# A macaron block with a selective scan: g^T of both FFNs by vector transposes and DRAM, softplus from its table, a new order

## The chip, the cores and the metric

The kernel runs on one core of one Trainium2 chip. Its engines are TensorE (PE, with PEld for its weight loads), VectorE (DVE), ScalarE (ACT), GpSimd (POOL) and SyncE (SP), which issues all DMAs here. The metric is the device time of one execution in microseconds (us), lower is better. Everything is float32.

## The reference, cut to what matters

The input x is [2, 2048, 1024]: 4096 rows of 1024. Three residual blocks follow each other:

```python
def ffn(x, A, B, W, bias):                       # A [64,16,1024], B [64,1024,16], W [1024,1024]
    vecs = einsum('arh,bsh->bsar', A, x)         # 64 vectors of 16 for each row
    _, idx = top_k(norm(vecs, axis=-1), 4)
    routes = one_hot(idx, 64).sum(-2) / 4        # 4 of 64 entries are 1/4
    v = einsum('bsa,bsar->bsr', routes, vecs)    # 16 numbers for each row
    delta = einsum('bsa,ajr,bsr->bsj', routes, B, v)
    return einsum('bsh,jh->bsj', x, W) + bias + delta

x = x + 0.5 * ffn(layernorm(x))
x = x + attn(layernorm(x))       # delta = softplus(x Wx Wdt + b_dt), then a scan over time:
                                 # h = exp(delta*A) * h + delta*B*x,  y = sum_n h*C, + x*D
x = x + 0.5 * ffn(layernorm(x))
```

The last term of the FFN is a product: with g[row, (r, a)] = v[row, r] * routes[row, a], a row of 1024 numbers, delta = g · wb, where wb is B laid out as [1024, 1024].

## The kernel before, in words

**Tiles.** The rows are cut into 16 chunks of 256 (`TC`), each of two row tiles of 128 (`P`). Every tile passes the first FFN (`ffn("f", c, i)`), every chunk the scan's preparation and the scan (`prepare(c)`, `scans(c)`), and every tile the second FFN (`ffn("g", c, i)`): 64 FFN tiles in all. Each takes three products of [128x1024] by [1024x1024] with the weights wa, ww and wb, which stay in SBUF. One tile's product by one weight is 16 products in the code and 32 matmuls of 128x512 in the profile.

**One FFN tile.** PE multiplies wa into the two banks `pv`; ACT squares them (`square`, L631); DVE sums the squares by route, finds the four largest and marks them (`choose`, L645 to L652), multiplies the marks into the vectors (`routed`, L658) and sums them to v (`total`, L668). POOL forms g from marks and v (`spread`, L677). `turn` transposes g in eight blocks of 128x128 on PE (L560) into two banks, and ACT copies them to `gt` (L565). PE meanwhile multiplies ww into the two banks `po` and then adds gt times wb (L578); `close` (L695) adds the result to the rows on DVE. There is one `g` tile and one `gt` tile.

**Softplus.** `prepare` has PE multiply `wdt` into a bank for two groups of 256 columns at a time (`pz`, L797). ACT takes |z| and max(z, 0) from it (L806, L807), then exp(-|z|) (L819) and, with the other function table, a logarithm (L833); DVE has four passes between them that keep the precision (L822, L827, L830, L836). The result `delta` and its product with x go to DRAM (`put`, L856). `scans` reads each row back eight times side by side (`rep`, L890), ACT forms the decays (L917), DVE the entries and scans (L925, L932), POOL multiplies by C and adds (L945, L964), and PE sums the states (L974).

**The order.** `add` records each step as a task with an engine, an assumed cost, what it reads and writes, the buffers that it takes and gives back (`Place`), and a rank. `Plan.order` plays the tasks through once when the program is built: an engine that is free takes the ready task of the lowest rank, and a DMA's data count as there after an assumed `land`. The order in which tasks begin there is the order in which each engine's instructions are written, and each engine keeps to it on the chip. So an assumed cost has no effect on the chip but through the order. For example:

```python
add("SP", 0.4, put_bc, [(bc, 0)], [(bc_d, 0)], rank=-45.3, take=[bc_d], give=[bc], land=1.2)
```

The products with ww and wb of a tile come when they are ready, ahead of the next tile's wa, by the number of their turn (`products`).

Of the kernel before, what the change touches and what calls it, by code (L numbers as in the profile page):

```python
# [16 lines left out]
P = 128  # L37
# [14 lines left out]

class Place:
# [10 lines left out]
class Task:  # L64
    __slots__ = (
        "eng", "cost", "emit", "rank", "take", "give", "port", "land", "turn", "waits", "users", "n",
        "at",
# [9 lines left out]
class Plan:  # L77
# [15 lines left out]
    def add(  # L93
        self, eng, cost, emit, reads=(), writes=(), rank=0.0, take=(), give=(), port=False, land=0.0,
        turn=None,
    ):
        t = Task()
        t.eng, t.cost, t.emit, t.rank = eng, cost, emit, rank
# [27 lines left out]
    def order(self):  # L126
# [9 lines left out]
        def arrive(t):  # L136
            heapq.heappush(ready[t.eng], (t.rank() if callable(t.rank) else t.rank, t.n))
# [89 lines left out]
def macaron_kernel(  # L227
# [54 lines left out]
    places("stats", 6, [P, 17])  # L282
    places("choice", 2, [P, NA + len(PADS) + RANK])
# [4 lines left out]
    plan.pool("du_d", [dram.tile([D, 2, TC], FP, name=f"du_d{j}") for j in range(6)])  # L288
# [32 lines left out]
    pads = const.tile([P, len(PADS) + 1], FP, name="pads")  # L321
    less = pads[:, len(PADS) :]
    nc.gpsimd.memset(less, -1.5)
    for j, v in enumerate(PADS):
        nc.gpsimd.memset(pads[:, j : j + 1], v)

    marked = []
    for j in range(2):
        norms = const.tile([P, NA + len(PADS)], FP, name=f"norms_{j}")
        nc.gpsimd.tensor_copy(norms[:, NA:], pads[:, : len(PADS)])  # L330
        tops = const.tile([P, 2, 8], FP, name=f"tops_{j}")
        nc.gpsimd.tensor_copy(tops[:, 1, :TOPK], pads[:, :TOPK])
        marked.append((norms, tops))
    plan.pool("marked", marked)
# [72 lines left out]
    def load_all():  # L407
        def one(dst, src, key, us, rank):
            keys = [(*key, h) for h in range(2)] if isinstance(key, tuple) else [key]
            add("SP", us, lambda: nc.sync.dma_start(out=dst, in_=src), [], keys, rank=rank, land=3.6)  # L410

        def big(w_sb, w, name, rank):
# [10 lines left out]
            rank=-1000.0, take=[mean_w])  # L423
# [17 lines left out]
        for w_sb, name, key in ((wa, "wa", "pv"), (ww, "ww", "po")):  # L441
            total = Place("row" if name == "wa" else "delta")
            for k in range(1, KC):
                def gather(k=k, w_sb=w_sb, total=total):
                    t = flat(total)
                    eng = nc.vector if total.pool == "row" else nc.gpsimd
                    eng.tensor_add(t, w_sb[:, 0, :] if k == 1 else t, w_sb[:, k, :])

                add("DVE" if name == "wa" else "POOL", 1.01 if name == "wa" else 2.45, gather, [(name, 0, 0), (name, k, 0)], [(total, 0)], rank=-1000.0,
                    take=[total] if k == 1 else [], port=True)  # L450
# [17 lines left out]
            for h in range(2):  # L468
# [10 lines left out]
                for k in range(KC):  # L479
# [4 lines left out]
                    add("DVE", 0.49, center, [(pt, 0)], [(name, k, h)], rank=-900.0, give=[pt])  # L484
# [6 lines left out]
            [], ["half_bias"], rank=272.6)  # L491
# [15 lines left out]
    def spread_of(x_p, st, factor, rank, after=()):  # L507
# [21 lines left out]
        def root():  # L529
            hv, r, t, q = (st.tile[:, j : j + 1] for j in (14, 15, 16, 12))  # L530
# [5 lines left out]
        add("DVE", 1.95, stats, row(x_p) + list(after), [(st, 0)], rank=-109.8 + rank, take=[st])  # L536
        add("ACT", 2.64, root, [(st, 0)], [(st, 1)], rank=72.4 + rank)

    def normalize(x_p, xn_p, rank, after=()):
# [4 lines left out]
        def scale():  # L544
            r, s = st.tile[:, 15:16], st.tile[:, 16:17]
# [6 lines left out]
    def turn(src, keys, dst, out_keys, rank, take=(), give_src=None):  # L552

        for g in range(2):
# [9 lines left out]
            def act(g=g, pt=pt):  # L564
# [4 lines left out]
                give=[src] if give_src else [])  # L569
            add("ACT", 0.58, act, [(pt, 0)], out_keys(g), rank=-111.3 + rank, give=[pt])  # L570
# [3 lines left out]
    def products(turn_of, ps, h, lhs, w, wn, start, stop, order, take, give, after=()):  # L574
        for k4 in range(KC // 4):
            def pe(k4=k4):
# [12 lines left out]
                [(ps[h], 0)], turn=turn_of, rank=order, take=take if k4 == 0 else (), give=give)  # L589

    def ffn(kind, c, i):
# [9 lines left out]
        g_p, gt, ch, mk, st = (Place(k) for k in ("g", "gt", "choice", "marked", "stats"))  # L601
# [11 lines left out]
        for h in range(2):  # L613
# [4 lines left out]
            add("POOL", 1.12, bias, row(x_p, h) + ["half_bias"], row(x_p, h), rank=rank, port=True)  # L618
# [7 lines left out]
        for h in range(2):  # L626
# [3 lines left out]
            def square(h=h):  # L630
# [7 lines left out]
                take=[g_p] if h == 0 else [])  # L638

        def choose():  # L640


            norms, tops = mk.tile
            routes = ch.tile[:, : NA + len(PADS)]
# [5 lines left out]
                out=routes, in_to_replace=tops[:, :, :TOPK], in_values=norms, imm_value=CHOSEN  # L650
            )
            nc.vector.tensor_scalar(routes, routes, CHOSEN, 1.0 / TOPK, ALU.is_equal, ALU.mult)  # L652

        add("DVE", 2.35, choose, [(g_p, 0), (g_p, 1)], [(ch, 0)], rank=-73.6 + rank,
            take=[ch, mk], give=[mk])
        for h in range(2):
            def routed(h=h):
# [3 lines left out]
                    ch.tile[:, :NA].unsqueeze(1).to_broadcast([P, r2, NA]),  # L661
                )

            add("DVE", 0.62, routed, [(pv[h], 0), (ch, 0)], [(g_p, h)], rank=-232.8 + rank,
                give=[pv[h]])

        def total():
            nc.vector.tensor_reduce(  # L668
                ch.tile[:, NA + len(PADS) :],
                g_p.tile.rearrange("p (r a) -> p r a", a=na), AX.X, ALU.add,  # L670
            )

        add("DVE", 1.2, total, [(g_p, 0), (g_p, 1)], [(ch, 1)], rank=-45.5 + rank)
        for h in range(2):
            def spread(h=h):
                v0 = NA + len(PADS) + h * r2
                nc.gpsimd.tensor_mul(  # L677
                    g_p.tile[:, h * HD : (h + 1) * HD].rearrange("p (r a) -> p r a", a=na),
                    ch.tile[:, :NA].unsqueeze(1).to_broadcast([P, r2, NA]),
                    ch.tile[:, v0 : v0 + r2].unsqueeze(2).to_broadcast([P, r2, NA]),  # L680
                )

            add("POOL", 0.99, spread, [(ch, 0), (ch, 1)], [(g_p, h)], rank=-27.7 + rank, port=True,
                give=[ch])
        turn(g_p, lambda g: [(g_p, g)], lambda g: gt.tile[:, g * HC : (g + 1) * HC, :],
             lambda g: [(gt, g)], rank, take=[gt], give_src=True)
# [3 lines left out]
        for h in range(2):  # L690
            products(turn_of, po, h, gt, wb, "wb", False, True, lambda: turn_of.number - 1000.0, [], [gt])

            def close(h=h):
# [7 lines left out]
                rank=-286.1 + rank, give=[po[h], st])  # L701
        if kind == "f":
            x1_ds[c, i] = x1_d = Place("x1_d")

            def keep():
# [3 lines left out]
                land=2.5)  # L709
# [11 lines left out]
    def prepare(c):  # L721
# [48 lines left out]
        def keep(p, pt, m):  # L770
# [4 lines left out]
            give=[pd])  # L775
        add("PE", 0.93, project_bc, ["wx"] + u_all, [(pb, 0)], rank=-79.8 + rank, take=[pb])
        add("ACT", 0.46, keep(bc, pb, P), [(pb, 0)], [(bc, 0)], rank=-138.9 + rank, take=[bc],
            give=[pb])
        add("PE", 0.36, fold, [(bc, 0)], [(pf, 0)], rank=91.8 + rank, take=[pf])
        add("ACT", 0.54, keep(bc, pf, 2 * N), [(pf, 0)], [(bc, 0)], rank=104.1 + rank, give=[pf])  # L780
# [8 lines left out]
        for g in range(2):  # L789
            dg, e = Place("delta"), Place("row")  # L790
            for k2 in range(HC // 2):
                pt = Place("bank")

                def pz(g=g, k2=k2, pt=pt):
                    for k in range(2):
                        kc = g * HC + 2 * k2 + k
                        nc.tensor.matmul(  # L797
                            pt.tile[:, k * TC : (k + 1) * TC], lhsT=wdt[:, kc * P : (kc + 1) * P],
                            rhs=dr.tile, start=True, stop=True,
                        )  # L800

                def parts(g=g, k2=k2, pt=pt, e=e, dg=dg):
                    for k in range(2 * k2, 2 * k2 + 2):
                        bias = bdt[:, g * HC + k : g * HC + k + 1]
                        z = pt.tile[:, k % 2 * TC : (k % 2 + 1) * TC]
                        nc.scalar.activation(e.tile[:, k * TC : (k + 1) * TC], z, AF.Abs, bias=bias)  # L806
                        nc.scalar.activation(dg.tile[:, k, :], z, AF.Relu, bias=bias)  # L807

                add("PE", 1.01, pz, [(dr, 0), "wdt"] + ([(e, "-")] if k2 else []), [(pt, 0)],
                    rank=-186.8 + rank, take=[pt] if k2 else [pt, e, dg], give=[dr])  # L810
                add("ACT", 1.95, parts, [(pt, 0), "bdt"], [(e, k2), (dg, k2)], rank=66.7 + rank,
                    give=[pt])
            ek, dk = [(e, k) for k in range(HC // 2)], [(dg, k) for k in range(HC // 2)]

            def flat(dg):
                return dg.tile.rearrange("p k t -> p (k t)")

            def exp(e=e):
                nc.scalar.activation(e.tile, e.tile, AF.Exp, scale=-1.0)  # L819

            def plus(e=e, dg=dg):
                nc.vector.scalar_tensor_tensor(  # L822
                    flat(dg), flat(dg), -1.0, e.tile, ALU.mult, ALU.subtract
                )

            def one(e=e):
                nc.vector.tensor_scalar_add(e.tile, e.tile, 1.0)  # L827

            def rest(e=e, dg=dg):
                nc.vector.scalar_tensor_tensor(flat(dg), e.tile, -1.0, flat(dg), ALU.add, ALU.add)  # L830

            def log(e=e):
                nc.scalar.activation(e.tile, e.tile, AF.Ln)  # L833

            def delta(e=e, dg=dg):
                nc.vector.tensor_sub(flat(dg), e.tile, flat(dg))  # L836
# [6 lines left out]
            add("ACT", 1.15, exp, ek, ek, rank=-3.2 + rank)  # L843
            add("DVE", 1.41, plus, ek + dk, dk, rank=-132.6 + rank, port=True)
            add("DVE", 0.92, one, ek, ek, rank=-214.4 + rank, port=True)
            add("DVE", 1.19, rest, ek + dk, dk, rank=-159.7 + rank, port=True)
            add("ACT", 3.62, log, ek, ek, rank=11.7 + rank)
            add("DVE", 1.21, delta, ek + dk, dk, rank=-94.7 + rank, port=True, give=[e])
            add("DVE", 1.07, times, dk + ukeys, ukeys, rank=-43.2 + rank, port=True, give=[dg])
# [230 lines left out]
```

## Time and profile before

| what | value |
|---|---|
| time, median of 3 runs | 3109.58 us (3109.41 to 3114.28) |
| span of the profiled execution | 3105.1 us |
| granted TensorE clock, mean | 0.998 |
| instructions | 36153 |
| DMA | 408160 packets, 476.37 MB, 52.6% of 16 engines' span |

Of the profiled execution itself the span is what is known, from the first to the last instruction; the median of the runs lies 4.5 us over it. "Busy" is the time in which an engine executes; the idle time of a group is what the engine stood still just before that group's instructions, followed by who released it. A line number such as L578 is that of the kernel before; the changed kernel has other numbers.

### The profile page before, as it was taken

What the parts mean: (1) busy time and instruction counts of PE and PEld (TensorE: products, weight loads), DVE (VectorE), ACT (ScalarE), POOL (GpSimd) and SP (SyncE); (2) the same over time, 40 slices, a digit from 0 to 9 for tenths busy, and PEclk for the clock granted to TensorE, in tenths of its full rate; (3) what the DMA queues carried; (4) which work ended last, traced back from release to release, by engine and by line L of the source; (5) the groups of instructions that cost most, each with busy time, mean ns of one, the idle gap of its engine ahead of it and who ended that gap; (6) DMA issues with size and microseconds to landing.
All of it is one profiled execution on the core that took longest, in us unless ns stands there. A gap on an engine that the chain in (4) does not pass through costs nothing.

```text
span 3105.1 us, 36153 instructions
## 1 busy us (share of the span) xinstructions
PE 3054.2 (98%) x9020; PEld 1409.4 (45%) x9020; DVE 2816.7 (91%) x4683; ACT 1869.4 (60%) x4851; POOL 2364.5 (76%) x1882
## 2 busy tenths in 40 slices
PE   8999999999999999999999999999999999999999
PEld 3444444444444444444444444444444444444444
DVE  4279999999999999999999999999999999997951
ACT  1366666656666676666566665666557675565531
POOL 3148787888788788788887887878888788886861
PEclk9999999999999999999999999999999999999999
DMA  5154654646465465555555555555465555544630
GB/s 226 61 167 147 194 146 138 195 142 190 130 183 157 145 181 163 154 159 163 166 172 150 165 162 164 166 166 169 133 172 168 166 161 148 160 143 130 170 81 14
DMA packets 408371, 478.69 MB, mean 154 GB/s; under 512 B 161504, under 2 KB 253280, under 8 KB 408160
## 3 DMA queue, kind: packets, MB, share of 16 engines
q1 hardware_dynamic: 408160, 476.37, 52.6%
q8 instruction: 72, 1.18, 0.2%
q14 instruction: 139, 1.14, 0.1%
HBM read 375.07 MB, written 101.19 MB: 153 GB/s over the span
## 4 chain that ended last, share of the span: by engine, by line
PE 60%; DVE 24%; issue 6%; ACT 4%; DMA 2%; POOL 2%; SPq 0%; DVEq 0%; POOLq 0%; ACTq 0%
PE bank L578 53%; DVE h L932 10%; DVE h L925 5%; PE bank L974 2%; PE bank L560 2%; PE bank L748 1%; POOL h L945 1%; DVE g L658 1%; ACT da L917 1%; DVE norms L645 1%; PE bank L797 1%; DVE stats L512 1%; DMA rep<-du_d 1%; DVE choice L652 1%; DVE bank L988 1%
## 5 line engine op out<-in xcount | busy, mean ns | idle before, releaser
L945 POOL TENSOR_TENSOR h<-h,c 128x512 f32<-128x512 f32 x1024 | 1323.7, 1303 | 351.8 <-ACT state L942 316.8
L917 ACT ACTIVATE da<-rep,a_neg 128x256 f32<-128x256 f32 x2048 | 974.8, 477 | 725.4 <-DVE h L932 675.6
L932 DVE TENSOR_TENSOR_SCAN h<-da,state,h 128x256 f32<-128x256 f32 x2048 | 1404.8, 731 | 7.3 <-ACT da L917 5.5
L578 PE MATMUL bank<-wa,xnt 128*128 128x512 f32 x2048 | 905.6, 596 | 5.4 <-DVE wa L482 4.0
L578 PE MATMUL bank<-wb,gt 128*128 128x512 f32 x2048 | 895.9, 595 | 10.0 <-ACT gt L565 9.8
L578 PE MATMUL bank<-ww,xnt 128*128 128x512 f32 x2048 | 889.4, 592 | 0.0
L964 POOL TENSOR_TENSOR h<-h,h 128x512 f32<-128x512 f32 x512 | 654.7, 1279 | 40.1
L925 DVE TENSOR_TENSOR h<-rep,b 128x512 f32<-128x512 f32 x1024 | 670.2, 665 | 12.5 <-ACT b L879 6.7
L578 PEld LDWEIGHTS bank<-ww,xnt 128*128 128x128 f32 x2048 | 389.1, 190 | 489.8 <-issue 483.4
L578 PEld LDWEIGHTS bank<-wb,gt 128*128 128x128 f32 x2048 | 384.4, 190 | 485.2 <-issue 453.5
L578 PEld LDWEIGHTS bank<-wa,xnt 128*128 128x128 f32 x2048 | 384.9, 191 | 483.4 <-issue 470.8
L677 POOL TENSOR_TENSOR g<-choice 128x512 f32<-128x512 f32 x128 | 143.5, 1142 | 195.8 <-DVE choice L668 195.8
L942 ACT COPY state<-h 128x2 f32<-128x2 f32 x1024 | 187.9, 185 | 54.5 <-DVE h L932 53.3
L631 ACT ACTIVATE g<-bank 128x512 f32<-128x512 f32 x128 | 133.8, 1047 | 87.9 <-PE bank L578 55.6
L512 DVE BATCH_NORM_STATS2 stats<-xf 128x6 f32<-128x512 f32 x128 | 81.2, 676 | 57.4 <-DMA xf<-in_x 57.4
L616 POOL TENSOR_TENSOR xf<-xf,half_bias 128x512 f32<-128x512 f32 x64 | 81.1, 1287 | 66.4 <-DVE stats L512 66.3
L974 PE MATMUL bank<-h,summer 128*32 128x512 f32 x1024 | 123.1, 598 | 0.0
L645 DVE TENSOR_REDUCE norms<-g 128x64 f32<-128x1024 f32 x64 | 77.0, 1203 | 50.8 <-ACT g L631 49.4
L533 ACT ACTIVATE stats<-stats,pads 128x1 f32<-128x1 f32 x288 | 111.3, 387 | 9.7
L565 ACT COPY gt<-bank 128x512 f32<-128x512 f32 x128 | 71.4, 592 | 66.9 <-PE bank L560 66.4
L695 DVE SCALAR_TENSOR_TENSOR xg<-bank,stats,xg 128x512 f32<-128x512 f32 x64 | 47.4, 741 | 67.6 <-PE bank L578 67.2
L532 ACT ACTIVATE stats<-stats 128x1 f32<-128x1 f32 x288 | 58.1, 202 | 81.8 <-DVE stats L527 75.7
(84 smaller groups left out, 1969.2 us busy)
## 6 DMA issues: line engine op xcount, KB each, us to landing
rep<-du_d SPq DMA_DIRECT2D x1024, 256.0 KB, 3.7
xnt<-in_x_t SPq DMA_DIRECT2D x32, 512.0 KB, 4.1
xf<-in_x SPq DMA_DIRECT2D x32, 512.0 KB, 5.4
x_d<-xf SPq DMA_DIRECT2D x32, 512.0 KB, 3.3
u_d<-u SPq DMA_DIRECT2D x32, 512.0 KB, 4.7
ysb<-u_d SPq DMA_DIRECT2D x64, 256.0 KB, 3.4
du_d<-delta SPq DMA_DIRECT2D x32, 512.0 KB, 3.2
du_d<-u SPq DMA_DIRECT2D x32, 512.0 KB, 3.5
```

What stands on the lines that cost most here:

```text
L512: nc.vector.bn_stats(st.tile[:, 6 * s : 6 * s + 6], x_p.tile[:, s * HD : (s + 1) * HD])
L533: nc.scalar.activation(t, q, AF.Identity, bias=less, scale=hv)
L578: nc.tensor.matmul(ps[h].tile, lhsT=lhs.tile[:, k, :], rhs=w[:, k, h * HD : (h + 1) * HD], start=start and k == 0, stop=stop and k == KC - 1,)
L631: nc.scalar.activation(g_p.tile.rearrange("p (a r) -> p r a", r=RANK)[:, h * r2 : (h + 1) * r2, :], vecs(pv, h), AF.Square,)
L677: nc.gpsimd.tensor_mul(g_p.tile[:, h * HD : (h + 1) * HD].rearrange("p (r a) -> p r a", a=na), ch.tile[:, :NA].unsqueeze(1).to_broadcast([ ...
L917: nc.scalar.activation(da.tile[:, k, :], r.tile[:, k, 0, :], AF.Exp, scale=a_neg[:, q + k, j, hi : hi + 1],)
L925: nc.vector.tensor_mul(h.tile, r.tile[:, :, 1, :], bs[hi].tile.unsqueeze(1).to_broadcast([P, 2, TC]),)
L932: nc.vector.tensor_tensor_scan(h.tile[:, k, :], da.tile[:, k, :], h.tile[:, k, :], state[:, q + k, j, hi : hi + 1], ALU.mult, ALU.add,)
L942: nc.scalar.copy(state[:, q : q + 2, j, hi : hi + 1], h.tile[:, :, TC - 1 : TC])
L945: nc.gpsimd.tensor_mul(h.tile, h.tile, cs[hi].tile.unsqueeze(1).to_broadcast([P, 2, TC]))
L964: nc.gpsimd.tensor_add(first.tile, first.tile, h.tile)
L974: nc.tensor.matmul(y.tile[j // 2 * 2 * DB : (j // 2 + 1) * 2 * DB, :], lhsT=summer[:, DB * (1 - j % 2) : DB * (3 - j % 2)], rhs=sums[j].ti ...
```

## The change

- **g^T.** DVE no longer turns the marks into 1/4 and 0: `choose` leaves -5 where a route is chosen, and ACT makes 1/4 of it (`mark`). The marks and v stand side by side in `rv` (128 x 96). DVE transposes it in blocks of 32x32 into `rvt`. Four DMAs write the blocks to DRAM so that `rv_d` is [96, 128]: a row for each route and each element of v. One DMA reads the 64 rows of routes twice into `rt` (128 partitions), two read the rows of v into `gt`, each row spread over 64 partitions. POOL multiplies rt into gt. The transposes of g, their banks and the ACT copies are gone.
- **Softplus** is one ACT function over four groups of 256 columns that wait in two banks; the four DVE passes are gone.
- **delta and u in DRAM** are laid out by partition, so that one DMA reads the `rep` of two column groups (4 KB a row) where two read 2 KB each.
- **Single buffers** for rv, rvt, rt, norms and tops.
- **The order.** Each kind of task has a constant (`SHIFT`) added to its rank, from -1806 to 1624, so that the order of all engines is new. SHIFT is no time.

The core of the diff:

```diff
+SHIFT = {
...
+    "choose f": 816.8,
+    "mark f": -819.1,
+    "routed f": -463.8,
+    "sum f": -75.2,
+    "put_rv f": 293.4,
+    "fetch_rv f": 613.0,
+    "spread f": 126.0,
+    "products ww": 125.4,
+    "products wb": -284.7,
...
+    "put_rv g": -1243.0,
+    "fetch_rv g": -1145.1,
+    "spread g": 1306.4,
...
-            heapq.heappush(ready[t.eng], (t.rank() if callable(t.rank) else t.rank, t.n))
+            rank = t.rank() if callable(t.rank) else t.rank
+            heapq.heappush(ready[t.eng], (rank + SHIFT.get(t.tag, 0.0), t.n))
...
-            nc.vector.tensor_scalar(routes, routes, CHOSEN, 1.0 / TOPK, ALU.is_equal, ALU.mult)
...
+        def mark():
+            nc.scalar.activation(
+                rv.tile[:, :NA], rv.tile[:, :NA], AF.Relu, bias=less_one, scale=-1.0 / TOPK
+            )
...
+            nc.vector.transpose(rvt.tile, rv.tile)
...
+        def put_rv():
+            for b in range(P // 32):
+                nc.sync.dma_start(
+                    out=rv_d.tile[:, 32 * b : 32 * b + 32].rearrange("(m i) j -> i m j", i=32),
+                    in_=rvt.tile[32 * b : 32 * b + 32, :].rearrange("p (m j) -> p m j", j=32),
+                )
+
+        def fetch_rv():
+            nc.sync.dma_start(
+                out=rt.tile, in_=rv_d.tile[:NA, :].unsqueeze(0).to_broadcast([P // NA, NA, P])
+            )
+            vs = rv_d.tile[NA : NA + RANK, :].rearrange("(c h) t -> h c t", h=P // NA)
+            for h in range(P // NA):
+                nc.sync.dma_start(
+                    out=gt.tile[h * NA : (h + 1) * NA, :, :],
+                    in_=vs[h].unsqueeze(0).to_broadcast([NA, KC, P]),
+                )
+
+        add("SP", 1.7, put_rv, [(rvt, 0)], [(rv_d, 0)], rank=-177.0, take=[rv_d], give=[rvt],
+            land=2.3, tag=f"put_rv {kind}")
+        add("SP", 1.2, fetch_rv, [(rv_d, 0)], [(rt, 0), (gt, 0), (gt, 1)], rank=-177.0,
+            take=[rt, gt], give=[rv_d], land=2.5, tag=f"fetch_rv {kind}")
...
-        turn(g_p, lambda g: [(g_p, g)], lambda g: gt.tile[:, g * HC : (g + 1) * HC, :],
-             lambda g: [(gt, g)], rank, take=[gt], give_src=True)
...
+            def softplus(g=g, pts=pts, dg=dg):
+                for k in range(HC):
+                    nc.scalar.activation(
+                        dg.tile[:, k, :], pts[k // 2].tile[:, k % 2 * TC : (k % 2 + 1) * TC],
+                        AF.Softplus, bias=bdt[:, g * HC + k : g * HC + k + 1],
+                    )
+
+            add("ACT", 4.6, softplus, [(pt, 0) for pt in pts] + ["bdt"], [(dg, 0)],
+                rank=11.7 + rank, give=pts)
...
+                    rows = du_d.tile[j * DB : (j + 1) * DB, q : q + 2, :, :]
+                    nc.sync.dma_start(
+                        out=r.tile.rearrange("p k s t -> p (k s t)"),
+                        in_=rows.rearrange("d k s t -> d (k s t)").unsqueeze(1).to_broadcast(
+                            [DB, LO, 4 * TC]
+                        ),
+                    )
```

## The prediction

> **What bounds the kernel now.** I read the page's first part, then the table of stretches, then the groups by shape, then the waits, then the timeline of one row tile, then the DMA issues.
>
> First the page: TensorE works nearly without a hole, VectorE is second. Then two stretches of the middle (columns: the stretch, its length, then busy time of PE, PEld, DVE, ACT, POOL, the granted clock, DMA share, GB/s).
>
> ```profile
> PE 3054.2 (98%) x9020; PEld 1409.4 (45%) x9020; DVE 2816.7 (91%) x4683; ACT 1869.4 (60%) x4851; POOL 2364.5 (76%) x1882
> ```
>
> ```profile
> 1000.00:2000.00 1000.00, 990.60 (x2983) 457.55 (x2982) 977.12 (x1623) 651.09 (x1700) 823.53 (x653) 1.00 0.56 162
> 2000.00:3000.00 1000.00, 991.54 (x2931) 454.20 (x2930) 957.03 (x1576) 614.40 (x1604) 823.19 (x652) 1.00 0.54 153
> ```
>
> So PE is idle for 3105.1 - 3054.2 = 50.9 us in all, and DVE is the second bound in the middle. Now the groups that the change touches (busy, mean ns of one | idle of the engine before them), and the wait for g^T.
>
> ```profile
> L578 PE MATMUL bank<-wb,gt 128*128 128x512 f32 x2048 | 895.9, 595 | 10.0 <-ACT gt L565 9.8
> L560 PE MATMUL bank<-ident,g 128*128 128x128 f32 x512 | 73.3, 276 | 14.8 <-ACT state L942 3.6 <-ACT u L565 3.6 <-ACT xnt L565 3.0
> L565 ACT COPY gt<-bank 128x512 f32<-128x512 f32 x128 | 71.4, 592 | 66.9 <-PE bank L560 66.4
> L652 DVE TENSOR_SCALAR choice<-choice 128x68 f32<-128x68 f32 x64 | 42.9, 671 | 2.2
> L822 DVE SCALAR_TENSOR_TENSOR delta<-delta,row 128x1024 f32<-128x1024 f32 x32 | 44.7, 1398 | 12.6 <-ACT row L819 12.6
> L833 ACT ACT_TABLE_LOAD x32 | 41.1, 1283 | 0.6
> ```
>
> The transposes of g cost PE 73.3 us and stand beside 14.8 + 10.0 us of waiting: g^T is hardly ever late. The timeline of the last tile says why (start, length, what):
>
> ```profile
> 3070.30 1.45 PE L578 MATMUL bank<-wa,xnt 128*128 128x512 f32 x3
> 3071.59 13.90 PE L578 MATMUL bank<-ww,xnt 128*128 128x512 f32 x32
> 3076.32 1.22 DVE L668 TENSOR_REDUCE choice<-g 128x16 f32<-128x1024 f32 x1
> 3077.69 2.05 POOL L677 TENSOR_TENSOR g<-choice 128x512 f32<-128x512 f32 x2 [18.32 <-DVE choice L668]
> 3085.32 1.04 PE L560 MATMUL bank<-ident,g 128*128 128x128 f32 x8
> 3086.59 0.70 PE L578 MATMUL bank<-wb,gt 128*128 128x512 f32 x1 [0.24 <-ACT gt L565]
> ```
>
> wa ends at 3071.75, the sums at 3077.54 (5.8 us later), g at 3079.7, and PE is in the ww products until 3085.5. g lies ready for 5.6 us. Over all 64 tiles the trace gives 8.5 us (median) from wa's end to the sums' end and 10.9 to g's. That reserve is what the change spends. Last, the DMAs nearest to the new ones:
>
> ```profile
> rep<-du_d SPq DMA_DIRECT2D x1024, 256.0 KB, 3.7
> y_d<-ysb SPq DMA_DIRECT2D x64, 256.0 KB, 2.3
> yt<-y_d SPq DMA_DIRECT2D x256, 64.0 KB, 3.5
> c<-bc_d SPq DMA_DIRECT2D x32, 128.0 KB, 2.6
> bc_d<-part SPq DMA_DIRECT2D x16, 32.0 KB, 3.1
> ```
>
> **PE.** The 512 transposes go: -73.3 us, all of it on the engine that sets the end, and with them the 24.8 us of waits beside them, which are counted anew below. Products, projections and state sums are as many as before; pz only comes in groups of four. Base: 3105.1 - 73.3 - 24.8 = 3007.0 us, of which 2980.9 are work.
>
> **DVE.** Out: L652 42.9, and of softplus L822 44.7, L827 24.6, L830 40.1, L836 42.2: 194.5 us. In: 64 transposes of 128x96, between the smallest row (L527, 144 ns) and the 128x512 transpose (L991, 716 ns); by size near 220 ns, 14 us. DVE comes to 2636 us. It stays beside PE and gives nothing by itself, but it no longer nearly binds: the 977 of 1000 us fall to about 910.
>
> **ACT.** Out: L806 60.4, L807 61.0, L819 33.6, L833 33.8, the g^T copies 71.4, and by the new instruction order 58 table loads stand for 64 (6 x 1.283 = 7.7): 268 us. In: 128 softplus of 128x256 at the 474 ns of L806 and L807, 61 us (as low as the 370 ns of the L771 copy, or one table pass dearer; off the path either way), and 64 marks of 128x64, between L532 (202 ns) and the 128x256 copy of L879 (376 ns), 0.3 us each, 19 us. ACT falls to about 1681 us. Hidden behind PE; if that cover went, four softplus and two loads are 4.5 us where the old chain per half, with DVE, took about 13.
>
> **POOL.** The 128 spreads multiply a broadcast rt into gt: the row of that form is L945, 1303 ns for L677's 1142, +21 us, 2385 us in all. Not a bound.
>
> **SP and the DMA engines.** Out: 512 of the 1024 rep issues (one of 512 KB for two of 256). In: 64 x (4 + 3) = 448. The queue gets no longer. Packets in: 64 x (384 of 128 bytes + 1152 of 512 bytes) = 98,304; at the mean of all packets (52.6% x 16 x 3105.1 us / 408,160 = 64 ns, high for such small ones) 393 us on each of 16 engines, 12.7%, at most 65% with the 52.6% of now. Behind each put on SP stand, in the new order, mostly one rep load and then the fetch, which holds SP until the put has landed; behind it wait more rep loads and so DVE's entries. A rep is taken up every 3000/512 = 5.9 us, four are buffered, so a few us there are hidden; without that cover each would be DVE idle time, of which there are now about 370 us.
>
> **The new chain, the term that decides.** From wa's end to the first wb product, L:
> - square, choose, routed, sums: 5.8 us undisturbed, 8.5 in the median. Less L652 (0.25 in the quiet tile), plus mark with its two handovers to ACT and back (0.5), plus the transpose (0.2): 6.25 to 9. I take 7.4, since DVE is less crowded.
> - put: four issues, the yt row's 481 ns each, so the fourth starts 1.45 us in; landing 2.3 (y_d) to 3.1 (bc_d): 3.75 to 4.55, say 4.1.
> - fetch: three issues, the last 1.0 us in; landing 2.6 (c) to 3.7 (rep): 3.6 to 4.7. A batch of four yt loads took 3.45 to 7.3 us from first issue to last landing, 4.65 in the median. I take 4.7, the bulk of gt being nearest to rep; both ends are kept.
> - spread: 1.3, and 0.5 for what POOL is at (half a 1.3 us instruction at 80%).
> - handovers: 0.35.
> L = 7.4 + 4.1 + 4.7 + 1.8 + 0.35 = 18.35 us. All low ends (6.25, 3.75, 3.6, 1.04 as the quickest spreads of now) give 15; all high ends (9, 4.55, 7.3, 2.6) give 23.8.
>
> The cover is the PE work that the new order sets between a tile's last wa product and its first wb: 32 ww (889.4/2048 = 434 ns each, 13.9 us) and what else stands there at its rows' durations. I summed it for all tiles: 13.9 to 34.7, median 17.9. The order was laid with 1.7 + 2.3 us for the put and 1.2 + 2.5 for the fetch, 7.7; I have 8.8. What a given L overhangs the cover, summed over the tiles: 3 us for L = 16, 10 for 17, 36 for 18, 78 for 19, 129 for 20, 184 for 21, 241 for 22. For 18.35 about 50.
>
> The row for a broadcast load is c, 2.6 us, and 512-byte packets took 27 ns in the trace. The Trainium skill ("DMA: Bandwidth & Descriptors", Rules for kernel authors) says that a source whose leading dimension is a zero-stride broadcast of c copies keeps the DMA on at most c engines; rt's leads with 2. No run here shows it. By that rule 64 packets, 1.7 us, would lie ahead of gt's on two engines, L would be 20 and the time about 3140.
>
> **Sum.** 3007 + 50 = 3057 us of span. The median of the runs lies 4.5 us over the profiled span (3109.6 against 3105.1), so 3061, say 3060.0. What the measurement can tell from no change is about 0.2%, 6 us.
>
> **Rivals.**
> 1. Hidden wholly: L at most 17, 0 to 10 us of stall, 3012 to 3022. For it: DVE and POOL are emptier, and a PE that is late finds them waiting. Against: two trips through DRAM, eight handovers, and a cover laid for 7.7. Chance 0.20.
> 2. The forecast, L 17 to 19.2: 3022 to 3100. Chance 0.50.
> 3. The end moves by less than 6 us, L near 19.4: 0.06.
> 4. Slower: the fetch outlasts the cover. Its place is PE's queue ahead of the first wb product, its price 51 to 57 us for each us of L beyond 19.4, which is the point from which it decides. With the slowest yt batch (7.3) L is 21: 3007 + 184 + 4.5 = 3195. For it: rep traffic on the same engines (share 0.56), reps of 4 KB ahead of the fetch. Against: median landings of 2.6 to 3.7. Chance 0.24.
> That the change does not do what it says holds only for the tables: Softplus and Exp still swap, 58 loads for 64; worth 8 us of ACT, none of the path.
>
> **Range and chances.** 3012 (hidden) to 3150 (L = 20.2), which leaves out the slower half of rival 4 and little below. Faster 0.20 + 0.50 = 0.70, same 0.06, slower 0.24.
>
> **What would show it.** Right: PE busy near 2981, no matmul on ident with g, DVE near 2636, ACT near 1681; the one new PE wait is wb on POOL's gt, 30 to 80 us; put near 4, fetch near 5 us. Wrong: a wb wait over 100 us (L mis-sized; look at the landing of rt and gt); PE waiting in other rows (the new order, not the trip); DVE idle on rep (SP held by the fetch); softplus well over 0.5 us.

## The result, and the profile after

| kernel | median | runs | against before |
|---|---|---|---|
| before | 3111.64 us | 4 (3109.41 to 3114.28) | |
| changed | 3388.84 us | 4 (3384.9 to 3391.1) | 1.0887, interval 1.0872 to 1.0903 |

The changed kernel is 8.9% slower. The profiled execution has a span of 3387.9 us. The first part of its page, and the two stretches of the middle (the columns are the stretch, its length, busy time of PE, PEld, DVE, ACT and POOL, the granted clock, DMA share, GB/s):

```profile
PE 3100.4 (92%) x8508; PEld 1390.4 (41%) x8508; DVE 2702.6 (80%) x4556; ACT 1734.7 (51%) x4589; POOL 2344.9 (69%) x1881
```

```profile
1000.00:2000.00 1000.00, 911.69 (x2549) 411.52 (x2548) 861.86 (x1452) 572.80 (x1515) 742.64 (x594) 0.95 0.60 162
2000.00:3000.00 1000.00, 919.32 (x2503) 405.58 (x2502) 863.82 (x1432) 522.66 (x1394) 777.82 (x622) 0.96 0.59 155
```

Two things are to be seen. PE is idle for 287.5 us, where it was 50.9. And with 512 instructions fewer it is busy for *longer* than before (3054.2), at a granted clock of 0.95 and 0.96 in the two stretches, where it was 1.00. So the work that is left runs slower.

The groups by shape name the place (busy, mean ns of one | idle of the engine before them):

```profile
L648 PE MATMUL bank<-wb,gt 128*128 128x512 f32 x2048 | 997.6, 650 | 249.6 <-POOL gt L778 249.6
L902 ACT ACTIVATE delta<-bank,bdt 128x256 f32<-128x256 f32 x128 | 50.5, 474 | 14.5 <-PE bank L892 13.9
L724 ACT ACTIVATE rv<-rv,pads 128x64 f32<-128x64 f32 x64 | 22.2, 347 | 57.0 <-DVE rv L719 57.0
L748 DVE STREAM_TRANSPOSE rvt<-rv 128x96 f32<-128x96 f32 x64 | 17.8, 278 | 2.2
L778 POOL TENSOR_TENSOR gt<-gt,rt 128x512 f32<-128x512 f32 x128 | 159.3, 1265 | 420.6 <-DMA gt<-rv_d 417.7
```

Nearly all new idle time stands ahead of wb: 249.6 us, in 60 waits for 64 tiles, 4.2 us each on the mean. The spread that wb waits for (the last line) itself waits for the DMA. The wb matmuls, which come right after each wait, take 650 ns on the mean where they took 595; those of ww take 593. Against the prediction's base the span divides so:

3387.9 - 3007.0 = 380.9 = 249.6 (wb's waits) + 119.5 (PE busy 3100.4 for 2980.9) + 11.8 (other idle, 37.9 for 26.1).

One tile shows both. First PE's timeline, then the granted clock in stretches of 3.4 us at the same place:

```profile
2652.36 13.90 PE L648 MATMUL bank<-ww,xnt 128*128 128x512 f32 x32
2666.18 1.92 PE L1037 MATMUL bank<-h,summer 128*32 128x512 f32 x16
2668.04 1.09 PE L629 MATMUL bank<-ident,xg 128*128 128x128 f32 x8
2673.39 16.35 PE L648 MATMUL bank<-wb,gt 128*128 128x512 f32 x32 [4.26 <-POOL gt L778]
```

```profile
2665.60:2669.00 3.40, 3.40 (x26) 1.26 (x24) 3.30 (x6) 2.42 (x7) 2.74 (x3) 1.00 1.12 195
2669.00:2672.40 3.40, 0.13 (x2) 0.00 (x0) 3.23 (x10) 2.97 (x10) 0.33 (x1) 0.84 0.48 115
2672.40:2675.80 3.40, 2.41 (x3) 1.17 (x4) 3.19 (x6) 2.41 (x8) 3.40 (x4) 0.50 0.53 173
2675.80:2679.20 3.40, 3.40 (x6) 1.39 (x5) 1.63 (x3) 1.19 (x5) 3.32 (x3) 0.65 0.73 174
2679.20:2682.60 3.40, 3.40 (x9) 1.52 (x8) 0.00 (x0) 0.00 (x0) 3.32 (x4) 1.00 0.45 119
```

Between wa and wb lie 13.9 + 1.9 + 1.1 us of other work; then PE waits 4.26 us. While it waits the clock falls to one half, and it stays there while wb begins: 3 and 6 matmuls in stretches that hold 9 at full clock. The product takes 16.35 us instead of 13.9. The trace's own records of the clock give the half clock from 2671.3 to 2678.2 us, so until 4.8 us after wb began.

These records also say how much of the 119.5 us is the clock. In the changed kernel there are 50 stretches at half clock, 286.7 us in all, and PE works for 212.3 us of them; before there were 3, 13.7 us, with 12.2 us of work. Two wb matmuls begin 853 ns apart there in the median, 429 ns at full clock. Half of the 200.1 us of additional slow work, about 100 us, is thus the clock's share by this estimate; what the other 19 us are was not found out. The chain of waits tells what filled the 21 us from wa to wb (start, length, what; DMA is the time from an issue to its data's arrival; "..." marks lines left out):

```profile
2661.38 1.50 DMA rv_d<-rvt
...
2663.03 0.52 SPq L761
...
2663.64 0.60 SPq L766
...
2664.29 7.66 DMA gt<-rv_d
...
2672.07 1.28 POOL gt L778
...
2673.39 26.65 PE bank L648 x56
```

The largest piece is the 7.66 us from the last issue to the arrival. Over all 64 tiles the medians, from wa's end, are: mark done 4.5, transpose done 7.9, put begins 8.1, fetch begins 11.4, spread begins 20.9, first wb product 22.1.

### The profile page after: what moved, and what is told of

Its sections match the earlier page's. It is cut to its first block, busy times and chain, and to the rows that moved or that the text cites. A ratio compares the mean times of both kernels' runs of the same rounds, so it can differ in the third digit from the quotient of the medians.

```text
span 3387.9 us, 34280 instructions
## 1 busy us (share of the span) xinstructions
PE 3100.4 (92%) x8508; PEld 1390.4 (41%) x8508; DVE 2702.6 (80%) x4556; ACT 1734.7 (51%) x4589; POOL 2344.9 (69%) x1881
## 3 DMA queue, kind: packets, MB, share of 16 engines
q1 hardware_dynamic: 439008, 517.26, 56.1%
## 5 line engine op out<-in xcount | busy, mean ns | idle before, releaser
L1008 POOL TENSOR_TENSOR h<-h,c 128x512 f32<-128x512 f32 x1024 | 1296.5, 1278 | 442.4 <-ACT state L1005 381.2
L648 PE MATMUL bank<-wb,gt 128*128 128x512 f32 x2048 | 997.6, 650 | 249.6 <-POOL gt L778 249.6
L648 PEld LDWEIGHTS bank<-wb,gt 128*128 128x128 f32 x2048 | 422.5, 209 | 810.3 <-issue 522.9
L778 POOL TENSOR_TENSOR gt<-gt,rt 128x512 f32<-128x512 f32 x128 | 159.3, 1265 | 420.6 <-DMA gt<-rv_d 417.7
L1005 ACT COPY state<-h 128x2 f32<-128x2 f32 x1024 | 171.9, 181 | 0.2 <-DVE h L995 0.2
L792 DVE SCALAR_TENSOR_TENSOR xf<-bank,stats,xf 128x512 f32<-128x512 f32 x64 | 47.5, 743 | 121.8 <-PE bank L648 121.2
L715 DVE TENSOR_REDUCE norms<-g 128x64 f32<-128x1024 f32 x64 | 77.2, 1206 | 58.2 <-ACT g L703 56.1
L687 POOL TENSOR_TENSOR xg<-xg,half_bias 128x512 f32<-128x512 f32 x64 | 80.9, 1270 | 37.3 <-PE bank L629 37.3
```

Source lines behind the costliest of these rows:

```text
L648: nc.tensor.matmul(ps[h].tile, lhsT=lhs.tile[:, k, :], rhs=w[:, k, h * HD : (h + 1) * HD], start=start and k == 0, stop=stop and k == KC - 1,)
L715: nc.vector.tensor_reduce(norms[:, :NA], g_p.tile.rearrange("p (a r) -> p a r", r=RANK), AX.X, ALU.add)
L778: nc.gpsimd.tensor_mul(part, part, rt.tile.unsqueeze(1).to_broadcast([P, HC, P]))
L1005: nc.scalar.copy(state[:, q : q + 2, j, hi : hi + 1], h.tile[:, :, TC - 1 : TC])
L1008: nc.gpsimd.tensor_mul(h.tile, h.tile, cs[hi].tile.unsqueeze(1).to_broadcast([P, 2, TC]))
```

## Experiments

Theory A came from the trace: rt's load (128 packets of 512 bytes) was spread over two DMA engines only, so 64 packets queue on each, at 42.7 ns each in this trace. The count of 4-byte packets fits. Before, the 1774 DMAs have 16 semaphore packets each, and two small loads have 2048 more packets of this size: 30,432, as counted. In the changed kernel 28,512 are counted for 1710 DMAs, which is 64 x 14 fewer than by this sum: each load of rt has 2 semaphore packets instead of 16. The main rival was that the trip through DRAM has a fixed length that no form of the loads shortens. In the table the waits, the busy time and the clock are those of one profiled execution. "Cover" is below, as in the prediction, the PE work between a tile's last wa product and its first wb.

| run | median, us | against before | wb's waits on gt, us | PE busy, us | clock |
|---|---|---|---|---|---|
| changed | 3388.84 | 1.0887 | 249.6 | 3100.4 | 0.958 |
| rt by two DMAs | 3238.03 | 1.0406 | 132.8 | 3061.4 | 0.975 |
| v in 4 KB runs | 3398.38 | 1.0922 | 254.1 | 3105.9 | 0.956 |
| both | 3236.79 | 1.0405 | 130.6 | 3063.8 | 0.975 |
| planned landing 9.0 | 3295.85 | 1.0592 | 111.9 | 3071.6 | 0.969 |
| filler products | 3359.47 | 1.0797 | 39.5 | 3279.9 | 0.995 |
| two DMAs, landing 4.4 | 3227.88 | 1.0372 | 76.8 | 3045.7 | 0.981 |
| two DMAs, landing 5.8 | 3207.24 | 1.0310 | 68.7 | 3045.1 | 0.980 |
| two DMAs, order searched | 3100.37 | 0.9958 | 8.7 | 3007.2 | 0.993 |
| one DMA, order searched | 3116.00 | 1.0015 | 20.7 | 3009.9 | 0.992 |
| softplus alone, in before | 3117.93 | 1.0021 | (g^T by PE) | 3057.1 | 0.995 |

**rt by two DMAs.** Each half of rt's partitions is loaded by a DMA of its own; the order of the other instructions stays.

```diff
-            nc.sync.dma_start(
-                out=rt.tile, in_=rv_d.tile[:NA, :].unsqueeze(0).to_broadcast([P // NA, NA, P])
-            )
+            for h in range(P // NA):
+                nc.sync.dma_start(out=rt.tile[h * NA : (h + 1) * NA, :], in_=rv_d.tile[:NA, :])
```

> The routes (rt) are read by two DMAs of 64 partitions each instead of one DMA whose source leads with a broadcast of 2; order of instructions as in the changed kernel. Theory A (rt runs on two DMA engines, and its packets and gt's queue up there): the thin tail of 512-byte packets after the bulk, 1 to 2.7 us in the trace, goes; L falls from 22.1 to about 19.5, the wait of the first wb product from 250 to about 110 us, the lost clock in proportion (119 to about 55 us): time 3390 - 140 - 65, about 3185, between 3140 and 3240. Theory B (the trip is long because of the rep loads ahead of it or the number of packets in all, not the two engines): the wait stays over 220 us, time 3350 or more.

Measured 3238.03 us, ratio 1.0406 (1.0385 to 1.0428): 151 us back with one more issue in each tile. The group of wb, and the same piece of the chain in a middle tile:

```profile
L648 PE MATMUL bank<-wb,gt 128*128 128x512 f32 x2048 | 953.7, 626 | 132.9 <-POOL gt L777 132.8
```

```profile
1638.49 4.25 DMA gt<-rv_d
```

From the last issue to the spread it is now 4.8 us in the median, for 8.0, though the issue comes 0.6 us later; from the first issue of the fetch to the spread 6.7, for 9.3; the first wb comes 20.1 us after wa. The span fell by 151.0: 116.8 of waits and 39.0 of PE time, less 4.8 of other idle. So in this order the two engines cost about 150 of the 381 us. The rest stays. The rival is refuted as to rt's load; a rest of 6.7 us from fetch to spread did not go.

**v in 4 KB runs.** The other small packets are gt's. With v's rows laid so that each partition of gt reads 4 KB in one piece (and wb's rows to match), 1024 packets of each fetch become 128.

```diff
-            vs = rv_d.tile[NA : NA + RANK, :].rearrange("(c h) t -> h c t", h=P // NA)
+            vs = rv_d.tile[NA : NA + RANK, :].rearrange("(h c) t -> h (c t)", h=P // NA)
```

> The rows of v lie in DRAM so that each partition of gt is one run of 4 KB instead of 8 runs of 512 bytes (wb's rows laid out to match); rt as in the changed kernel, same order. Theory A (two engines with 64 packets of rt and 64 of gt each are the tail): gt's 64 packets of 512 bytes on an engine (42 ns, 2.7 us) become 8 of 4 KB (225 ns, 1.8 us), L falls by about 0.9 to 21.2, the wait to about 195 us, time about 3310 (3270 to 3350). Theory B (the number of packets in all decides): 1152 packets become 256, L falls by 2 us or more, time under 3250.

Measured 3398.38 (1.0922, 1.0899 to 1.0944), waits 254.1 us, first wb at 22.1 as before. Neither theory's gain came: gt's packets set nothing as long as rt's come last.

**Both edits.**

> rt by two DMAs of 64 partitions (all 16 engines) and gt in runs of 4 KB, order as in the changed kernel. Theory A (with the two-engine tail gone, gt's 64 packets of 512 bytes on each engine are the bulk of the fetch, 42 ns each, 2.7 us, against 8 of 4 KB at 225 ns, 1.8 us): L from 19.9 to about 19, the wait from 133 to about 95 us, time about 3190 (3170 to 3215). Theory B (what is left is the fixed part of two trips and the queue behind the rep loads): 3238 within 15 us.

Measured 3236.79 (1.0405, 1.0384 to 1.0426), fetch to spread again 6.7 us. The time is the rival's. So even with rt spread over all engines, the size of gt's packets made no difference. What is left of the trip does not hang on these packets; what it hangs on was not measured further.

**A later landing in the plan.** Only the number with which the order is laid is changed, 2.5 to 9.0 us for the fetch; no instruction is.

> Only the number by which the order is laid is changed: the fetch is assumed to land 9.0 us after its issue instead of 2.5, so that PE's order puts more work between a tile's last wa product and its first wb (median 25.8 us for 17.9). All instructions stay. Theory A (the loss is the overhang of the trip over its cover, and the clock that falls because of it): with L = 22 the overhang is 28 us, the clock stays at full speed, the time is about 3045 (3020 to 3090). Theory B (the order anew and the single buffers cost by themselves): other waits take the place, time over 3200.

Measured 3295.85 (1.0592, 1.0571 to 1.0614). The cover between wa and wb grew from 17.9 to 25.8 us in the median, as theory A meant, and the waits on gt fell by more than half. But the spread came later too: first wb at 28.8. PE's waits of this run:

```profile
PE bank L648 <- POOL gt L778: 111.9, 32, 16.0
PE bank L648 <- ACT xnt L634: 27.0, 21, 3.4
```

From the fetch to the spread it is 12.1 us, while POOL waits for the DMA for 118.3 us in all, where it was 417.7. So in most tiles the data lie there and POOL, which takes the tasks as the plan has them, is at something else. xnt comes late more often as well, 27.0 us in all. The time is the rival's (over 3200), and so is part of its claim: moving one number moved much of the wait to the next queue.

**Filler products.** Five products of 128x512 that add zero stand before each tile's first wb; they wait for nothing.

```diff
+                if wn == "wb" and h == 0 and k4 == 0:
+                    for _ in range(5):
+                        nc.tensor.matmul(
+                            ps[h].tile, lhsT=ident, rhs=zeros[:, :1].to_broadcast([P, HD]), start=False, stop=False
+                        )
```

> The changed kernel with five products of ident with zeros (10 matmuls, 4.3 us, they add 0) ahead of each tile's first wb product; they do not read gt, so PE runs them while it would wait. Theory A (PE's busy time rose from 2981 to 3100 us because the waits let the granted clock fall): the clock goes back to about 1.0, the idle of wb on gt to under 60 us, and the time falls by about the 119 us of the clock, to 3270 (3240 to 3310), although 278 us of useless work are added. Theory B (PE's extra busy time is no matter of the waits): the useless work only fills the waits and the time is 3380 or more.

Measured 3359.47 (1.0797, 1.0774 to 1.0819): 29 us *faster* than the changed kernel, with more work in it. Its page and its largest wait:

```profile
PE 3279.9 (98%) x9148; PEld 1477.2 (44%) x9148; DVE 2700.3 (80%) x4557; ACT 1735.1 (52%) x4589; POOL 2344.3 (70%) x1881
```

```profile
PE bank L655 <- POOL gt L785: 39.5, 24, 4.5
```

The 640 matmuls are worth 278 us at the 434 ns of a ww matmul; 3279.9 less that is 3002, for 3100.4. About 98 us of slow PE time went away with the idle time, at a clock of 0.995; the 100 us that the clock records gave are the same by another way. This is the run that shows the waits to be the cause of the half clock. The time lies between the two theories: theory A let the filler replace the waits at no cost, but it is 68 us longer than the waits that it took away. As a remedy it fails, since 278 us of filler stand in for 210 of waits.

**The corrected fetch with a moderate landing.** rt by two DMAs, and 4.4 or 5.8 us in the plan.

> rt by two DMAs (all 16 engines), and the order laid with 4.4 us for the fetch's landing instead of 2.5; median cover 21.0 us for 17.9. Theory A (overhang of L over the cover): with L = 19.9 the overhang is 42 us instead of 129, the clock near full, time about 3100 (3070 to 3140). Theory B (as in the run with 9.0: an order with a later fetch also puts POOL's spread later in POOL's queue, so L grows with the cover): the wait stays over 100 us, time 3190 or more.

> The same with 5.8 us, median cover 22.0. Theory A: overhang 20 us at L = 19.9, time about 3080 (3050 to 3120). Theory B: L grows beyond 22, time 3190 or more, and the spread starts well after its data have come.

Measured 3227.88 (1.0372, 1.0354 to 1.0390) and 3207.24 (1.0310, 1.0289 to 1.0330). Covers of 21.0 and 22.0 us, but first wb at 22.6 and 24.1. The second run's waits:

```profile
PE bank L648 <- POOL gt L777: 68.7, 32, 9.1
PE bank L648 <- ACT xnt L634: 40.4, 22, 5.8
```

The spread begins 18.6 us after wa with the landing of 2.5, then 20.7 and 22.4: of the 3.1 and 4.1 us of cover won, 2.1 and 3.7 are lost to a later spread. Part of that comes ahead of the fetch, which begins at 11.7, 13.2 and 13.5 us. xnt, 15.5 us with the old landing, becomes late as well. Both times are the rival's (3190 or more), though the wait of over 100 us that it named for the first did not come. With SHIFT left as it is, none of the landings tried made the trip fit.

**An order searched for the true trip.** The tasks' costs and landings were set to what the runs had shown (among others put 1.9 + 1.5, fetch 2.5 + 4.8, spread 1.27, project 3.6 us, and 4.3 us for rep's landing), and SHIFT was searched anew for the plan that ends first. The second kernel has the same order with rt by one DMA.

> The fetch of the routes goes out as two DMAs over all 16 engines, and the instruction order is laid anew throughout with costs and landings as the runs so far have measured them (put 1.9 + 1.5 us, fetch 2.5 + 4.8 us, spread 1.27, project 3.6). The PE work that this order sets between a tile's last wa product and its first wb product is 15.8 to 62.8 us, median 52.7 (17.9 in the changed kernel), so that most tiles have another tile's products in between; an L of 20 us overhangs it by 6 us over all tiles, 23 us by 19. Theory A (the loss is the trip's length over its cover, and the half clock follows from the waits): first wb's waits on gt under 20 us, the granted clock above 0.99, TensorE busy near 2990, time 3020 to 3090, faster than the kernel before. Theory B (work moved between the tiles only moves the wait: POOL's spread or DVE's sums come later by as much, or other rows wait): PE waits of over 120 us in sum, time over 3110.

> The same instruction order as in the run beside it, but rt is fetched by one DMA whose source leads with the broadcast of 2, as in the changed kernel. Theory A (cover decides, whatever the trip's length): the fetch takes some 2.6 us longer, L about 22.5, overhang of the covers 15 us, so within 0.7% of the run beside it, 3030 to 3110. Theory B (two engines cost also where the wait is covered, by holding the SP queue and the pools of gt and rt longer): more than 40 us above the run beside it.

Measured 3100.37 (0.9958, 0.9943 to 0.9973) and 3116.00 (1.0015, 1.0005 to 1.0025). The page, the waits and the PE timeline of the first:

```profile
PE 3007.2 (97%) x8508; PEld 1357.4 (44%) x8508; DVE 2697.8 (87%) x4556; ACT 1739.2 (56%) x4593; POOL 2354.9 (76%) x1881
```

```profile
PE bank L648 <- ACT xnt L634: 17.9, 10, 4.1
PE bank L629 <- ACT row L616: 17.4, 13, 2.9
PE bank L648 <- DMA xnt<-in_x_t: 17.0, 8, 3.2
PE bank L648 <- POOL gt L777: 8.7, 13, 1.1
```

```profile
1510.82 7.13 PE L648 MATMUL bank<-ww,xnt 128*128 128x512 f32 x16
1517.79 7.03 PE L648 MATMUL bank<-wb,gt 128*128 128x512 f32 x16
1524.65 7.03 PE L648 MATMUL bank<-ww,xnt 128*128 128x512 f32 x16
```

wb is split among ww products in halves, and most tiles have another tile's products between their wa and their wb: a cover of 52.7 us in the median. The wait on gt is gone (8.7 us), no single wait is longer than 4.2 us, and the clock is 0.993. Theory A holds on these counts, and its time is missed by 10 us: PE is busy for 3007.2 instead of 2990 and idle for 86.6 us in the rows shown and smaller ones. By this run's page the chain of work that ended last goes through DVE for 52% of the span and through PE for 25% (before: 24% and 60%), so that PE alone no longer sets the end. Against before the span is 11.3 us shorter: 47.0 less work, 35.7 more waiting. One DMA for rt costs 15.6 us here, where it cost 151 in the order of the changed kernel: with a long cover the form of the load matters little, as theory A had it (its bounds in us were 6 us too low). This kernel is faster than the changed one and, by 0.4%, than the one before. Whether the same search would help the kernel before, which idles for 50.9 us, was not tried.

**Softplus alone.** The kernel before with the new softplus and nothing else; one cost, of the product after it, is set so that the order can be laid.

> The kernel before, with softplus as one table function over a bank's two groups of 256 columns in place of the seven steps on ACT and DVE; g^T by PE as before; the order is laid with an assumed 5.8 us for the product with u so that it stays near the old one. Theory A (PE bounds; DVE and ACT work of softplus is hidden): PE busy unchanged near 3054, DVE down by 152 us, time within 15 us of before (3095 to 3125). Theory B (softplus itself costs, by its table or by the order): over 3130. Theory C (DVE was the second bound in the middle): under 3095.

Measured 3117.93 (1.0021, 1.0011 to 1.0031). DVE is busy for 2683.1 us for 2816.7 and ACT for 1829.1 for 1869.4 (in this order it loads a table 119 times, where it was 65), and the time does not follow. What is taken from the two engines beside PE is hidden, as the prediction said. The 0.2% may be the order; that was not tested.

## Why the prediction was wrong

The main line had the trip nearly hidden, 50 us of overhang. Its rival 4 named the right place and the right mechanism (the fetch outlasts the cover) and was given 0.24. Two things failed: the fetch in the sum, too short, and the clock, which was not in the sum at all. The span of 3387.9 us lies 330.9 over the 3057 of the sum: 199.6 of additional waits of wb, 119.5 of slower PE work and 11.8 of other idle time.

- **The fetch, 4.7 us in the chain L, took 9.3.** This is the step that failed; even the slowest batch that the prediction had looked at (7.3 us) was shorter. The 4.6 us missing have three parts: 0.3 for the issues (the third begins 1.3 us in, for 1.0); 1.1 for the landing on 16 engines, 4.8 us from that issue to the spread in the run with two DMAs where rep's 3.7 stood (rep itself, now 512 KB at a time, landed in 4.9 there); and 3.2, 8.0 less 4.8, for rt on two engines. The last had been weighed and left out. The Trainium skill ("DMA: Bandwidth & Descriptors", Rules for kernel authors) says that a DMA whose source leads with a broadcast of c copies is kept on at most c engines. This case agrees: 2 semaphore packets for each load of rt instead of 16, and 151 us back with two loads. The prediction priced it by the 27 ns that 512-byte packets had taken before, 1.7 us. But that was the mean of 128 packets of one single load, 38 us into the kernel; here the mean is 42.7 ns over 73,856. Even with the 1.7 us in its sum the forecast would have been about 3140.
- **The rest of L was nearly right.** Transpose done at 7.9 (7.4 said), then 0.2 to the put, the put 3.3 (4.1), the spread 1.3 with no delay on POOL in the median (1.8), first wb at 22.1 for 18.35. Apart from the fetch the terms differ by -0.85 us in sum.
- **The overhang came out.** The prediction's table gives 241 us for L = 22 and some 6 more for 22.1; measured 249.6. So close a fit is partly luck, since the first wb came between 17 and 34 us after wa and not at one L. Summing PE's work between wa and wb tile by tile is the part of the method to keep.
- **The clock was missing.** The base took 2980.9 us of PE work as given. With a wait of 4.2 us in most tiles it became 3100.4. So each us of waiting cost 119.5 / 249.6 = 0.48 us more, and the price per us of L was, by this estimate, near 80 instead of 51 to 57. The trace of before shows no wait over 2.0 us from 110 to 3000 us, and there the clock was below full once, for 3.4 us. The Trainium skill ("TensorE: Matmul & The Clock Gate", Part 1) states that the array falls to half clock after an idle window of some 3.4 us and needs as long a busy one to return. The trace agrees with a fall, to 0.50 during the wait of 4.26 us shown, but not with the length: 12 of the 50 falls came without any wait over 3.4 us in the 3.4 us before, the shortest after 2.05 us. Of the 10 waits of 1 to 2 us none was followed by half clock, of the 13 of 2 to 3 us 7, of the 45 longer ones 44. The return came 4.6 us after work began again in the median (2.8 to 6.2).
- **DVE 2636 said, 2702.6 measured; ACT 1681 and 1734.7.** DVE's rows came nearly as said: its groups sum to 2999.7 us before and 2823.9 after, 176 less for 180.5 forecast. But a group's busy time overlaps its neighbours' in the same engine, and the union, which the page gives, fell by 114.1 only. Off the path, it cost nothing.
- **Right:** softplus hidden (by the run with softplus alone) and at 474 ns, 58 table loads (29 and 29), mark 347 ns for 0.3 us, no transposes of g, DMA share 56.1%, under the bound of 65%. The transpose of 128x96 took 278 ns for 220.
- **Rival 1, "hidden wholly"**, did not come in this order. The searched order comes near it (8.7 us of waits on gt), and its 3093.8 us of span are 87 over the base of 3007, in other waits (60.5) and slower PE work (26.3). So even there the 73 us of transposes bring 11.

## What to carry to other kernels

When a step leaves the bounding engine for a longer way round, compare the length of the way, tile by tile, with the work that the order puts in its place; that work is in the instruction lists before anything runs. Add the price of the clock to waits of more than 2 us (in this trace), and make the landing times those of the loaded kernel with the form of each access pattern looked at, not those of a quiet row. And lay the order with what the trip measures: here the same instructions took 3388.8 or 3116.0 us by the order alone.

## What was not expected of the hardware

- A wait of 4.26 us on PE took the granted clock to 0.50, and it was back at 1.00 only 4.8 us after work began again; a wait of 2.05 us was enough once. Together with 60 waits on gt PE's work grew by 119.5 us. Useless matmuls of 278 us in their place made the kernel 29 us faster.
- The 512-byte packets took 42.7 ns each, and 38.2 with rt on all engines; those of 4096 bytes took 225 ns, for 184 before. These are not the same transfers: before, rep moved in packets of 2048 bytes, and only one load had any of 512. So the runs do not show how much of the difference is load.
- Landing times differ widely within one kernel: with rt on all engines the small writes of a put (12 KB each) had landed after 1.5 us in the median, the reads of gt (256 KB) after 4.4, of rep after 4.9 and of xf after 7.1 (both 512 KB). x_d, a write of 512 KB, landed after 3.2. What sets them was not tested.
